# Codebook convolutions on TensorE: softmax numerators in 32-row array tiles, with patches assembled in DRAM

## The chip, the cores and the metric

The kernel runs on one core of a Trainium2 chip, float32 throughout. The metric is the device time of one execution in microseconds (us). Where a kernel ran once, its run's state can't be told; runs of two or more here are in the fast state.

## The reference, cut to what matters

Sixteen images of 256 channels and 28 x 28 pixels go through group norm and two 3 x 3 convolutions in which each channel's patch of nine taps is replaced by a softmax over 16 codes:

```python
p = patches(x)                                  # b, pixel, channel, 9 taps
d = sum(p*p) - 2 * p @ centroids + sum(centroids**2)    # b, pixel, channel, 16 codes
attn = softmax(-d, axis=-1)
lut = einsum('cks,cso->cko', centroids, w_sub)  # channel, code, 256 outputs
out = einsum('bnck,cko->bno', attn, lut)
# conv 1: relu(bn(.)); conv 2: bn, squeeze-excite gate; then relu(out + x); then + x
```

The term |p|^2 is the same for all codes and cancels in the softmax. There are 32 *stages*: 16 images by two convolutions.

## The kernel before

A unit is 8 channels by 448 or 336 pixels. Logits have pixels on the partitions, so the maximum and the sum over the codes are reductions along the free axis. The attention weights must then be transposed before the lookup. Patches go from SBUF to SBUF.

```python
def logits(u):
    for i in range(nt):     # 73 rows: a row of ones, 9 taps x 8 channels
        nc.tensor.matmul(lg[:PP, i * P : (i + 1) * P], lhsT=pt[:, k, c0 : c0 + PP],
                         rhs=wd[l][:, g, :], start=True, stop=True)
    nc.vector.tensor_reduce(mx, lv, axis=AX.X, op=ALU.max)
    nc.vector.tensor_tensor(zv, lv, mx..., ALU.subtract)
    nc.scalar.activation(z, z, AF.Exp, scale=2.0)
def normalise(u):
    nc.vector.tensor_reduce(sm, zv, axis=AX.X, op=ALU.add)
    nc.vector.reciprocal(sm, sm)
    nc.gpsimd.tensor_tensor(zv, zv, sm..., ALU.mult)
def transpose(u):
    for i in range(nt):
        nc.tensor.transpose(tp[:, i * PP : (i + 1) * PP], z[:, i * P : (i + 1) * P], ident[:PP, :PP])
    nc.scalar.copy(at, tp)
def lookup(u):
    for o in range(NB):     # 128 (channel, code) rows against a table made in the setup
        nc.tensor.matmul(acc[o, hi], lhsT=lut[l][:, g, o * P : (o + 1) * P], rhs=u["at"], ...)
# ... cut: setup of the table, norms, gate, the order of the stream
```

## Time and profile before

| | before |
|---|---|
| time | 5238.65 us (two runs, 5236.41 and 5240.88) |
| TensorE busy | 98% |
| DMA engines busy (main queue) | 13.8% |
| DRAM read, written | 17.90 MB, 12.85 MB |

In these lines each digit is a fortieth of the run in tenths, PEclk is the clock granted to TensorE, and the queue's columns are packets, MB and its share of 16 engines' time:

```profile
PEclk9999999999999999999999999999999999999999
DMA  1111111111111111111111111111111111111110
...
q1 hardware_dynamic: 124480, 278.29, 13.8%
...
HBM read 17.90 MB, written 12.85 MB: 6 GB/s over the span
```

The transfers are nearly idle and hardly touch DRAM.

### The profile page before, as it was taken

The numbers are of one execution on the slowest core, as the hardware profiler recorded it, in microseconds if no ns is written. First come the engines' busy times: TensorE is split into PE (matmuls) and PEld (weight loads), VectorE is DVE, ScalarE is ACT, GpSimd is POOL, SyncE is SP. The second block draws the span as 40 slices with busy tenths as digits, with TensorE's granted clock in tenths as the row PEclk, the third lists the DMA queues.
The fourth block names the chain that finished last, engine by engine and source line by source line (L and its number), as shares of the span: only waits on it lengthen the run. The fifth ranks groups of instructions, "written<-read, shape, count | busy, mean of one in ns | idle before, by whom it ended". The sixth has DMA issues, their size and how long they took to land.

```text
span 5236.6 us, 94950 instructions
## 1 busy us (share of the span) xinstructions
PE 5144.1 (98%) x30112; PEld 3875.6 (74%) x30112; DVE 4102.7 (78%) x8497; ACT 2106.5 (40%) x4417; POOL 1944.8 (37%) x2105
## 2 busy tenths in 40 slices
PE   6899999999999999999999999999999999999999
PEld 2677777777777777777777777777777777777776
DVE  1778787878878788787888878788787887878787
ACT  2344434444434444434444444444344444344443
POOL 1333333333333333333333333333333333333333
PEclk9999999999999999999999999999999999999999
DMA  1111111111111111111111111111111111111110
GB/s 40 72 51 49 51 62 51 62 50 62 51 50 62 51 62 50 50 62 51 62 50 59 53 52 61 50 62 51 51 61 50 62 51 51 62 50 56 52 55 37
DMA packets 132931, 284.70 MB, mean 54 GB/s; under 512 B 45904, under 2 KB 50528, under 8 KB 132448
## 3 DMA queue, kind: packets, MB, share of 16 engines
q1 hardware_dynamic: 124480, 278.29, 13.8%
q8 instruction: 258, 4.23, 0.3%
q14 instruction: 225, 1.84, 0.1%
q10 hardware_dynamic: 7968, 0.34, 0.1%
HBM read 17.90 MB, written 12.85 MB: 6 GB/s over the span
## 4 chain that ended last, share of the span: by engine, by line
PE 91%; DVE 3%; DMA 2%; SPq 1%; ACT 1%; issue 1%; ACTq 1%; POOL 0%; DVEq 0%; POOLq 0%
PE acc L341 48%; PE lg L303 28%; PE tp L328 13%; DMA xt<-in_x_dram 2%; SPq L290 1%; PE ps L157 1%; ACT y L365 1%; ACTq L145 1%; DVE sm L320 1%; PE ps L164 1%; DVE mx L310 1%; DVE gn_st L196 0%; DVE z L313 0%; DVE y L275 0%; DVE sm L321 0%
## 5 line engine op out<-in xcount | busy, mean ns | idle before, releaser
L322 POOL TENSOR_TENSOR z<-z,sm 120x512 f32<-120x512 f32 (+1 forms) x2048 | 1904.9, 949 | 3133.2 <-DVE sm L321 2965.0
L341 PE MATMUL acc<-at,lut 128*128 128x448 f32 (+1 forms) x8192 | 2909.7, 494 | 6.4 <-ACT at L330 5.5
L341 PEld LDWEIGHTS acc<-at,lut 128*128 128x128 f32 x8192 | 1457.1, 190 | 885.9 <-issue 680.8
L314 ACT ACTIVATE z<-z 120x512 f32<-120x512 f32 (+1 forms) x2048 | 1087.9, 570 | 1994.2 <-DVE z L313 1960.3
L303 PE MATMUL lg<-wd,pt 73*120 73x128 f32 x14336 | 1765.5, 273 | 15.4 <-DMA pt<-xn 9.9
L310 DVE TENSOR_REDUCE mx<-lg 120x32 f32<-120x512 f32 (+1 forms) x2048 | 1240.6, 622 | 625.5 <-PE lg L303 624.7
L303 PEld LDWEIGHTS lg<-wd,pt 73*120 73x120 f32 x14336 | 1659.7, 183 | 54.0 <-issue 22.4
L320 DVE TENSOR_REDUCE sm<-z 120x32 f32<-120x512 f32 (+1 forms) x2048 | 1188.2, 614 | 345.7 <-ACT z L314 340.3
L330 ACT COPY at<-tp 128x448 f32<-128x448 f32 (+1 forms) x2048 | 916.9, 487 | 962.4 <-PE tp L328 960.6
L313 DVE TENSOR_TENSOR z<-lg,mx 120x512 f32<-120x512 f32 (+1 forms) x2048 | 1179.0, 612 | 2.7
L328 PEld LDWEIGHTS tp<-ident,z 120*128 120x128 f32 x7168 | 826.8, 141 | 287.3 <-issue 56.0
L328 PE MATMUL tp<-ident,z 120*128 120x120 f32 x7168 | 944.0, 266 | 7.2 <-POOL z L322 7.1
L321 DVE RECIPROCAL sm<-sm 120x32 f32<-120x32 f32 (+1 forms) x2048 | 537.9, 298 | 4.0
L157 PE MATMUL ps<-ws,wd 73*128 73x256 f32 x128 | 59.3, 650 | 42.4 <-DMA wd<-in_L_conv_centroids_dram 38.1
L162 DVE TENSOR_TENSOR sq<-wd 73x512 f32<-73x512 f32 x16 | 10.9, 688 | 98.2 <-PE ps L164 77.7
L157 PEld LDWEIGHTS ps<-ws,wd 73*128 73x128 f32 x128 | 33.9, 313 | 68.0 <-issue 44.3
L365 ACT ACTIVATE y<-acc,bnsh,bnsc 128x448 f32<-128x448 f32 (+1 forms) x64 | 42.7, 672 | 25.6 <-PE acc L341 25.6
L358 ACT ACTIVATE h<-acc,bnsh,bnsc 128x448 f32<-128x448 f32 (+1 forms) x64 | 41.6, 678 | 26.5 <-PE acc L341 26.5
L196 DVE BATCH_NORM_STATS2 gn_st<-xt 128x6 f32<-128x392 f32 x64 | 31.6, 555 | 24.4 <-DMA xt<-in_x_dram 24.4
L151 POOL MEMSET ws<- 1x2048 f32 x8 | 14.3, 1794 | 77.3 <-PE ps L157 70.5
L158 ACT COPY lut<-ps 128x256 f32<-128x256 f32 x64 | 23.7, 372 | 36.9 <-PE ps L157 31.0
L275 DVE SCALAR_TENSOR_TENSOR y<-y,se_gt,xn 128x784 f32<-128x784 f32 x32 | 37.8, 1185 | 0.6
(48 smaller groups left out, 236.7 us busy)
## 6 DMA issues: line engine op xcount, KB each, us to landing
pt<-xn SPq DMA_DIRECT2D x2304, 52.5 KB
pt<-h SPq DMA_DIRECT2D x2304, 52.5 KB
xt<-in_x_dram SPq DMA_DIRECT2D x16, 784.0 KB
out_dram<-y SPq DMA_DIRECT2D x16, 784.0 KB
ws<-in_L_conv_wsub_dram SPq DMA_DIRECT2D x72, 64.0 KB
wd<-in_L_conv_centroids_dram ACTq DMA_DIRECT2D x64, 4.5 KB
vecs<-in_L_conv_bn_gamma_dram ACTq DMA_DIRECT2D x2, 1.0 KB
vecs<-in_L_conv_bn_beta_dram ACTq DMA_DIRECT2D x2, 1.0 KB
```

Of the source, the lines that this page charges most:

```text
L157: nc.tensor.matmul(ps, lhsT=wdl[:, g, :], rhs=ws[:, qi, :], start=True, stop=True)
L303: nc.tensor.matmul(lg[:PP, i * P : (i + 1) * P], lhsT=pt[:, k, c0 : c0 + PP], rhs=wd[l][:, g, :], start=True, stop=True,)
L310: nc.vector.tensor_reduce(mx, lv, axis=AX.X, op=ALU.max)
L313: nc.vector.tensor_tensor(zv, lv, mx.unsqueeze(2).to_broadcast([PP, n, K]), ALU.subtract)
L314: nc.scalar.activation(z[:, : nt * P], z[:, : nt * P], AF.Exp, scale=2.0)
L320: nc.vector.tensor_reduce(sm, zv, axis=AX.X, op=ALU.add)
L321: nc.vector.reciprocal(sm, sm)
L322: nc.gpsimd.tensor_tensor(zv, zv, sm.unsqueeze(2).to_broadcast([PP, n, K]), ALU.mult)
L328: nc.tensor.transpose(tp[:, i * PP : (i + 1) * PP], z[:, i * P : (i + 1) * P], ident[:PP, :PP])
L330: nc.scalar.copy(at[:, : nt * PT].rearrange("p (r w) -> p r w", w=W), tp[:, : nt * PP].rearrange("p (r w) -> p r w", w=WP)[:, :, 0:W],)
L341: nc.tensor.matmul(acc[o, hi][:, : nt * PT], lhsT=lut[l][:, g, o * P : (o + 1) * P], rhs=u["at"][:, : nt * PT], start=u["first"], stop=u[" ...
L365: nc.scalar.activation(y[:, o, t0 * PT : (t0 + nt) * PT], a, AF.Identity, bias=sh[:, o : o + 1], scale=sc[:, o : o + 1], accum_out=ysum[:, ...
```

## The change

Its intent is to take TensorE, the bound, out of the transposes and of a third of the lookup's cost. Codes go on the partitions instead of pixels. Three channels (27 taps and helper rows) share a 32-row tile of the array, and eight tiles run at once. The exponentials are multiplied with the centroids to *softmax numerators* (27 taps and three sums in 32 rows), which sub-weights then turn into outputs, four tiles to a 128-row matmul. A maximum over codes now lies across partitions: a first pass of logits is turned in 32 x 32 blocks and reduced, the maxima go through DRAM into spare patch rows, and a second pass of logits subtracts them. The sums go out to DRAM, in again over 128 partitions, through a logarithm and an exponential for the reciprocal, out and in again. Patches are assembled in DRAM: three copies of the image (left, middle, right shift; `home`) are written, and nine transfers copy them into patch order (`pat`), from which tiles are loaded.

The diff, cut to its core (cuts are marked):

```diff
-            nc.tensor.matmul(lg[:PP, i * P : (i + 1) * P], lhsT=pt[:, k, c0 : c0 + PP], rhs=wd[l][:, g, :], ...)
-    nc.vector.tensor_tensor(zv, lv, mx.unsqueeze(2)..., ALU.subtract)
-    nc.tensor.transpose(...)          # and lookup(), the table's setup, im2col() in SBUF
 ...
+    def to_home(l, b, part):
+        if part == 0:
+            nc.sync.dma_start(view(dst, DX + W, [[NPAD, P], [P * NPAD, NB], [1, HW]]), src)
+            return
+        if dx == 0:
+            nc.sync.dma_start(view(dst, to + 1, [[NPAD, P], [W, H], [1, W - 1]]), img[:, :, 0 : W - 1])
+        else:
+            nc.sync.dma_start(view(dst, to, [[NPAD, P], [W, H], [1, W - 1]]), img[:, :, 1:W])
+    def to_pat(l, b, n):
+        nc.sync.dma_start(view(pat_of(l, b), base * HW, [[32 * HW, NRT], [step * HW, 3], [1, HW]]),
+            view(d_home[l], dx * DX + j * NPAD, [[3 * NPAD, NRT], [W, 3], [1, HW]]))
 ...
+    def logits(u, gi, first, rows, n):
+        for i in range(4):
+            for h in range(2):
+                nc.tensor.matmul(bs[i][64 * h : 64 * h + 64, :n],
+                    lhsT=wd[l][32 * i : 32 * i + rows, 2 * g + h, :],
+                    rhs=u["pt"][32 * i : 32 * i + rows, 2 * gi + h, first : first + n], start=True, stop=True)
+    def a_turn(u, gi):                # first pass
+            nc.vector.transpose(z[:, :n], u["lg", gi][i][:, :n])
+    def a_max(u, gi):
+            nc.vector.tensor_reduce(u["mx"]..., z..., axis=AX.X, op=ALU.max)
+    def m_out(u): ...                 # maxima to DRAM
+    def m_in(u): ...                  # and into rows 7, 15, 23 of each tile of pt
+    def b_exp(u, gi):                 # after the second pass
+            nc.scalar.activation(e[:, :n], bk[:, :n], AF.Exp, scale=2.0)
+    def b_num(u, gi):
+                nc.tensor.matmul(bs[h][32 * i : 32 * i + 32, :n], lhsT=cw[l][64 * h : 64 * h + 64, g, i, :],
+                    rhs=e[64 * h : 64 * h + 64, :n], start=True, stop=True)
+    def b_keep(u, gi): nc.scalar.copy(u["q"]..., bk[:, :n])
+    def s_out(u): nc.sync.dma_start(view(u["ds"], ...), u["q"][7::8, :m])
+    def s_in(u):  nc.sync.dma_start(u["sp"][:, :m], view(u["ds"], ...))
+    def r_make(u):
+        nc.scalar.activation(sp, sp, AF.Ln)
+        nc.scalar.activation(sp, sp, AF.Exp, scale=-1.0)
+    def r_out(u): nc.sync.dma_start(view(u["dr"], ...), u["sp"][:, :m])
+    def r_in(u):  nc.sync.dma_start(u["rt"][7::8, :m], view(u["dr"], ...))
+    def c_scale(u, gi):
+            nc.vector.stream_shuffle(rb[:, :n], u["rt"][:, a : a + n], MASK)
+            nc.gpsimd.tensor_tensor(u["q"][:, a : a + n], u["q"][:, a : a + n], rb[:, :n], ALU.mult)
+    def c_look(u, gi, o):
+            nc.tensor.matmul(accs[key][:, :n], lhsT=ws[l][:, 2 * g + h, o * P : (o + 1) * P], rhs=u["q"]..., ...)
 ... cut: the order of the slots, borders, norms, gate, constants
```

A *slot* is 24 channels by 384 or 400 pixels; there are 704. A *unit* of one or two slots is what the round trips work on; there are 384.

## The prediction

> **What bounds the kernel now.** I read the page's busy shares first, then the chain that ended last, then a stretch of that chain in order of time, then the groups.
>
> ```profile
> PE 5144.1 (98%) x30112; PEld 3875.6 (74%) x30112; DVE 4102.7 (78%) x8497; ACT 2106.5 (40%) x4417; POOL 1944.8 (37%) x2105
> PE acc L341 48%; PE lg L303 28%; PE tp L328 13%; DMA xt<-in_x_dram 2%; SPq L290 1%; PE ps L157 1%; ACT y L365 1%; ACTq L145 1%; DVE sm L320 1%; PE ps L164 1%; DVE mx L310 1%; DVE gn_st L196 0%; DVE z L313 0%; DVE y L275 0%; DVE sm L321 0%
> ```
>
> TensorE is both the busiest engine and 91% of the chain. A busy TensorE alone would prove little, but the chain in order of time closes without a gap:
>
> ```profile
> 2501.27 2.63 PE acc L341 x8
> 2503.90 0.72 PE tp L328 x7
> 2504.62 1.53 PE lg L303 x14
> 2506.15 2.64 PE acc L341 x8
> ```
>
> A period (two units: 8 channels, 784 pixels) is 2.63 + 0.72 + 1.53 = 4.88 us, all TensorE; 1,024 periods make 5.00 of the 5.24 ms. The rest is the setup (first logits start at 152 us) and the tail. From these lines come my TensorE rates. A float32 matmul is two instructions (8,192 for 4,096 lookups in the code), and the eight lookup instructions average 392 columns and 329 ns: 0.84 ns a column and instruction. The logits' 14 weight loads and matmuls of 120 to 128 columns go at 109 ns each.
>
> ```profile
> L310 DVE TENSOR_REDUCE mx<-lg 120x32 f32<-120x512 f32 x1024 | 704.5, 688 | 621.8 <-PE lg L303 621.0
> L310 DVE TENSOR_REDUCE mx<-lg 120x24 f32<-120x384 f32 x1024 | 569.3, 556 | 3.7 <-PE lg L303 3.7
> L320 DVE TENSOR_REDUCE sm<-z 120x32 f32<-120x512 f32 x1024 | 700.5, 684 | 330.6 <-ACT z L314 330.0 <-issue 0.2
> L322 POOL TENSOR_TENSOR z<-z,sm 120x384 f32<-120x384 f32 x1024 | 857.8, 838 | 100.3 <-DVE sm L321 41.2 <-PE lg L303 33.0 <-ACT z L314 24.5
> L314 ACT ACTIVATE z<-z 120x384 f32<-120x384 f32 x1024 | 522.0, 510 | 60.9 <-DVE z L313 58.0
> L330 ACT COPY at<-tp 128x336 f32<-128x336 f32 x1024 | 454.3, 444 | 199.1 <-PE tp L328 197.6 <-ACT at L330 0.2
> ```
>
> These give the other engines' costs at about 400 columns (the second number after the bar, in ns). VectorE costs 1.03 ns a column plus about 160 ns. It is second, at 78%: a change that only relieves TensorE can win at most to there.
>
> **What the Trainium skill says.** (1) "TensorE: Matmul & The Clock Gate", Part 3 on row and column tiling: matmuls in distinct tiles of the array run at once; sixteen 32x32 tiles measured 10.6 times. The same part says matmuls are strictly first in, first out in start and end. The trace of before can't confirm either: its large matmuls use 73 rows or more, hence no tiles. (2) "TensorEngine Tiling (Array Packing)", Key Properties: changing the tiling mode drains the engine. No trace here yet. (3) "VectorE: DVE Perf Modes", the perf-mode tier table: tensor_reduce and STREAM_SHUFFLE exist only at one element a cycle. The trace agrees for the reduce (688 ns for 512 columns). (4) "DMA: Bandwidth & Descriptors", anatomy of one DMA: about 2 us are fixed, mostly the write's receipt. The trace's issue and landing records of the patch transfers (52.5 KB) give a median of 2.8 us, so it agrees roughly.
>
> **The change part by part.** The unit of work becomes a slot: 24 channels (eight 32-row tiles of three) by 384 or 400 pixels. 32 stages x 2 pixel tiles x 11 slots = 704 slots. A slot is 1.5 old periods of work (7.33 us of old time). Padding to 264 channels makes the total 1,056 old periods' worth in place of 1,024.
>
> *TensorE, a slot.* Removed: the transposes (0.72 us a period) and the 73-row logits. The table lookup becomes four full 128x128 matmuls (8 instructions of 392 columns): 2.63 us, as eight do now. A table group held 8 channels in 128 rows; numerator rows hold 12 (nine taps each), so this costs 2.63 instead of 3.95 us. Added: logits twice (eight 31x64 tiles each, 400 and 392 columns) and numerators (eight 64x32 tiles): 24 matmuls, 48 instructions of about 0.33 us. One after the other they would be 15.8 us; the change lives on their running at once. If eight tiles run at once, each group takes two passes (0.66 us) or its weight loads, whichever is longer: 16 loads of 64 columns at 0.9 ns (109 ns for 120) are 0.9 us, of 32 columns 0.46 us. I take 1.0, 1.0 and 0.7 us. Four changes of tiling a slot at about 0.16 us (a matmul's 266 ns record less its 103 ns spacing in the transposes: the pipeline's length, an estimate) are 0.65 us. Sum: 2.63 + 2.7 + 0.65 = 6.0 us.
>
> *VectorE, a slot.* Removed: subtraction, sum, reciprocal. Kept: the maxima. Added: a 32x32 block transposition of every logit and the shuffles. Four transpositions of 400 columns from PSUM and four reductions, each 573 ns by the maxima's row, about 555 with the overlap of successors seen in the timeline (a pair takes 1.21 us for 1.24 of records): 4.4 us. Two shuffles at 0.53 us: 1.06. The transposition of the maxima (256 columns, 0.38 us a unit of 1.83 slots): 0.21. Sum 5.7 us; 704 slots make 4.0 ms, and 0.13 ms of norms and residuals stay.
>
> *ScalarE, a slot.* Four exponentials (517 ns at 392 columns), two copies (488 ns), logarithm and exponential for the reciprocal (about 0.4 us): 3.4 us. *GpSimd:* two products at 852 ns: 1.7 us. Neither bounds.
>
> *DMA.* The patch reads stay near 290 MB against 278 now. Assembling the patches in DRAM adds 238 MB (nine transfers of 828 KB a stage). Now 278 MB are 13.8% of the engines; after it perhaps 30%. Small pieces are cheap: 64-byte packets take 10 ns in the setup. What counts is latency: maxima go out and back (two landings), sums out and back, reciprocals out and back (four). At 2.8 us each these need 5.6 us in a window of about 1.6 slots (9.8 us), and 11 us in over four. Both fit, and the ends of the chains stand half a slot apart, which fits landings of 2.8 us and slots near 6 us.
>
> *Sum.* The slot is set by TensorE (6.0) and VectorE (5.7) side by side, with little left for the handover: VectorE must empty four of six banks before the second logits, and ScalarE those before the next first logits. I put 6.1 us on a slot: 704 x 6.1 = 4,294 us. The start (x in, norm, borders, nine assemblies, first patches; no table to make): about 80 us for 152 now. The tail (nine slots of lag with little in them, gate, store): 45 us. **4,420 us.**
>
> **The rivals.**
> *Tiles don't overlap enough.* The two instructions of one float32 matmul use the same tile, so the second must wait for the first. If starts are strictly in order, only the second of one tile overlaps the first of the next: 9 steps in place of 2 for a group, 3 us, and a slot is 3 x 3.0 + 2.63 = 11.6 us: 8.2 to 8.4 ms. For it: the skill's sentence on order. Against: the design itself, which would be pointless (it computes all logits twice), and its lags, which are cut for slots near 6 us. Issue itself is no obstacle:
>
> ```profile
> L243 PE MATMUL ps<-ysum,w_sb x8: 163/163/177, 2543.7 to 2543.9; 128*16 128x1 f32 x8
> ```
>
> Eight one-column matmuls with their loads start within 0.2 us: about 25 ns a pair.
> *VectorE is the bound.* With TensorE at 4.6 us (no load limit, cheap mode changes) the slot is 5.7 us: 4.0 + 0.13 + 0.12 = 4.15 to 4.25 ms. For it: its count is the surest part of the sum.
> *The round trips through DRAM are the bound.* All of them go through one queue that waits in order. The sums' part (out 2.8, in 2.8, reciprocal 1 to 2, out 2.8, in) is about 10 us for each unit of two slots, and an assembly transfer ahead delays it by some 3 us. A slot would then be 7 us and the time 5.0 ms. Against: the queue's parts interleave, and most slots have no assembly.
> *Logarithm and exponential need different tables.* Two loads of 1.28 us (the one in the trace of before) for 384 units are 0.98 ms on ScalarE: 3.4 ms busy. It would lengthen the slot only by its place in the chain, some 0.2 us.
>
> **Range and chances.** Most of the weight lies between the VectorE floor (4.15 ms) and round trips that bite (5.0 ms), so 4,050 to 5,300 us. About one in seven goes to tiles that hardly overlap, which is far outside. Hence faster 0.81, within 2% 0.03, slower 0.16.
>
> **What would show it.** Right: matmul groups of 16 records starting within about 1 us, a VectorE busy above 90%, TensorE's span per slot near 6 us, few waits on DMA. The spacing of successive tiled matmuls decides the first rival: near 60 ns it falls, near 330 ns every second one it holds. A block transposition above 0.6 us would put VectorE above TensorE; idle time of TensorE ended by a DMA before the second logits, or of VectorE before the shuffles, would show the round trips. More than one ACT_TABLE_LOAD shows the tables. The prediction is wrong at its root if the groups take 3 us.

## The result, and the profile after

The kernel after takes 6626.53 us (two runs, 6622.87 and 6630.20), with results that agree with the reference. The ratio to before is 1.265, 95% interval 1.2614 to 1.2687. Ratios are the mean time of one kernel's fast runs over that of the other's of the same rounds, so not quite the ratio of the medians. It is 26% slower, outside the range and in the other direction than predicted.

The page after, answering to the lines shown of before (busy shares, fortieths, queue, DRAM):

```profile
PE 4794.6 (72%) x39692; PEld 1742.8 (26%) x39692; DVE 3781.4 (57%) x9141; ACT 3072.5 (46%) x6034; POOL 1525.5 (23%) x1490
...
PE   0009777778687777977777787877779777777978
...
PEclk5558887889888888988888897887889788788989
DMA  1174777675767767586776758577675867767573
...
q1 hardware_dynamic: 1292484, 872.37, 64.4%
...
HBM read 672.02 MB, written 448.08 MB: 169 GB/s over the span
```

TensorE is now busy 72%, and the clock granted to it is 0.85 in the mean from 600 us on (0.99 in e5_none_one below, where it hardly pauses). No engine is near its limit. The first three digits of TensorE are 0: some 500 us pass before any logits. The main queue moves 3.1 times the bytes and holds the DMA engines 64% of the time. With no engine full, the time must lie in waits, so I looked first at a stretch in order of time, then at the waits in sum. First, one group of first-pass logits by itself (duration in ns as least, median, most; first and last start in us):

```profile
L353 PE MATMUL lg<-pt,wd x16: 481/506/532, 3001.3 to 3001.7; 31*64 31x384 f32 x16
```

Sixteen instructions of half a microsecond start within 0.4 us. The records behind it show eight starts 7 ns apart, then, 327 ns after the last of these, eight more: all first passes of the float32 matmuls, then all second ones. So the tiles do overlap, and the rival that held 14% falls. The stretch around it (start, duration, and in brackets the idle time before with what ended it):

```profile
2996.62 3.01 SPq L445 DMA_DIRECT2D ds<-q  x1
...
3001.28 0.90 PE L353 MATMUL lg<-pt,wd 31*64 31x384 f32 x16
3002.11 1.61 PE L489 MATMUL acc<-q,ws 128*128 128x400 f32 x4
3003.65 0.88 PE L427 MATMUL nm<-e,cw 64*32 64x384 f32 x16
3004.46 0.90 PE L353 MATMUL lg<-pt,wd 31*64 31x384 f32 x16
3005.29 1.61 PE L489 MATMUL acc<-q,ws 128*128 128x400 f32 x4
3008.90 0.34 SPq L450 DMA_DIRECT2D sp<-ds  x1
...
3011.95 0.37 ACT L455 ACTIVATE sp<-sp 128x200 f32<-128x200 f32 x1 [9.96 <-DMA sp<-ds]
...
3014.42 2.70 PE L353 MATMUL lg<-pt,wd 31*64 31x384 f32 x16 [7.52 <-ACT q L440]
```

From start to start, a slot is 0.83 (logits) + 1.54 (half the products with sub-weights) + 0.81 (numerators) + 0.83 + 1.54 = 5.55 us. That is the kernel as designed, better than the 6.1 I gave it. Then it stops. The sums sent out at 2996.62, right behind the last copy of an image, are in DRAM only at 3008.90, twelve microseconds later, where 2.4 us is the median. The packet records show what lay in front of them: the 108-byte packets of that image copy run from 2997.1 to 3005.6 us, and the first packet of the sums starts only at 3002.6. ScalarE has come to the logarithm in its program and waits 9.96 us for them. Behind the logarithm stand the copies and exponentials that empty PSUM banks, so TensorE has nowhere to write and idles 7.52 us; its next group then takes 2.70 us in place of 0.90.

How often that happens shows in the distances between the 704 numerator groups, worked out from the trace: the least 5% are at 5.50 us, the median 6.33, the highest quarter above 10.8, the highest 5% above 19.1, the mean 8.6. So nearly the whole loss is stalls on top of a good slot.

Not all of a stall is idle time. The trace grants TensorE either the full clock or half of it: half for 2,333 us of this run, for 603 us of e5_none_one, the start of some 500 us included in both. Two successive products that start at half clock are 666 ns apart at the median, at full clock 336. TensorE's busy time for the same 39,692 instructions is 4,795 us here and 4,091 there. So up to some 700 us of the loss (an estimate, the difference of these two) is TensorE working slowly, or waiting inside its groups, around stalls. The prediction, whose rates come from a run at a granted clock of 0.999, has no term for this.

The waits (in all, times, longest, in us):

```profile
ACT sp L455 <- DMA sp<-ds: 987.4, 218, 27.3
...
PE lg L353 <- DMA pt<-dm: 651.8, 146, 17.6
...
DVE rb L479 <- DMA rt<-dr: 640.1, 227, 16.4
...
PE lg L353 <- ACT q L440: 407.7, 117, 11.9
```

All three round trips (sums, maxima, reciprocals) are there, each with waits several times a landing. The groups of instructions tell that the engines' own costs are not to blame (the second number after the bar is the mean in ns):

```profile
L480 POOL TENSOR_TENSOR q<-q,rb 128x384 f32<-128x384 f32 (+1 forms) x1408 | 1404.4, 1019 | 4673.6 <-DVE rb L479 2482.8
L369 DVE STREAM_TRANSPOSE z<-lg 128x416 f32<-128x416 f32 (+1 forms) x2816 | 1437.5, 567 | 1552.6 <-PE lg L353 1549.4
...
L377 DVE TENSOR_REDUCE mx<-z 128x26 f32<-128x416 f32 (+1 forms) x2816 | 1394.5, 558 | 0.0
...
L455 ACT ACT_TABLE_LOAD x384 | 492.7, 1283 | 602.5 <-DMA sp<-ds 597.5
L479 DVE STREAM_SHUFFLE rb<-rt 128x384 f32<-128x384 f32 (+1 forms) x1408 | 768.7, 594 | 3.2 <-issue 1.1
```

I had taken 573, 573 and 530 ns for the three VectorE forms and 852 for GpSimd's. The table loads are the rival that I gave 0.2 us a slot: 384 before the logarithm and as many before its exponential, 985 us of ScalarE in all.

Which transfers hold the DMA engines follows from the trace's packet records. The left and right copies of the image write rows of 27 pixels, 108 bytes: 458,752 packets. Half of them take 13 ns or less, but 5% take over 184 and the mean is 46. These 49.5 MB, under 6% of the queue's bytes, are 19.9% of the span of the 16 engines, close to a third of all DMA work. One such copy of 378 KB is in place some 13 us after its issue. The first 500 us have the same look:

```profile
47.07 62.48 ACTq L127 DMA_DIRECT2D home<-zero  x2
126.17 5.58 SPq L263 DMA_DIRECT2D home<-xn  x1
211.05 69.05 ACTq L127 DMA_DIRECT2D home<-zero  x2
402.90 2.80 SPq L112 DMA_DIRECT2D xt<-in_x  x1
```

Border columns are cleared in single elements of 4 bytes, 7,392 to a transfer, and issuing two such transfers takes 62 and 69 us. Their packets go on longer: those of the first two run from about 49 to 192 us, 106 a microsecond over all engines, although the record of one packet is 7 ns long. So the duration of a packet alone doesn't price such a transfer. The image copies wait for the borders, and the load of the second image, which stands behind them in the same queue, is issued at 403 us.

### The profile page after: what moved, and what is told of

Its sections match the earlier page's. It is cut to its first block, busy times and chain, and to the rows that moved or that the text cites. A ratio compares the mean times of both kernels' runs of the same rounds, so it can differ in the third digit from the quotient of the medians.

```text
span 6628.5 us, 106293 instructions
## 1 busy us (share of the span) xinstructions
PE 4794.6 (72%) x39692; PEld 1742.8 (26%) x39692; DVE 3781.4 (57%) x9141; ACT 3072.5 (46%) x6034; POOL 1525.5 (23%) x1490
## 3 DMA queue, kind: packets, MB, share of 16 engines
q1 hardware_dynamic: 1292484, 872.37, 64.4%
## 5 line engine op out<-in xcount | busy, mean ns | idle before, releaser
L489 PE MATMUL acc<-q,ws 128*128 128x384 f32 (+1 forms) x5632 | 2534.8, 577 | 182.6 <-POOL q L480 181.7
L353 PE MATMUL lg<-pt,wd 31*64 31x384 f32 (+2 forms) x22528 | 1769.6, 573 | 1224.9 <-DMA pt<-dm 651.8
L480 POOL TENSOR_TENSOR q<-q,rb 128x384 f32<-128x384 f32 (+1 forms) x1408 | 1404.4, 1019 | 4673.6 <-DVE rb L479 2482.8
L369 DVE STREAM_TRANSPOSE z<-lg 128x416 f32<-128x416 f32 (+1 forms) x2816 | 1437.5, 567 | 1552.6 <-PE lg L353 1549.4
L418 ACT ACTIVATE e<-lg 128x400 f32<-128x400 f32 (+1 forms) x2816 | 1183.8, 517 | 779.0 <-PE lg L353 778.0
L489 PEld LDWEIGHTS acc<-q,ws 128*128 128x128 f32 x5632 | 1063.5, 210 | 1662.7 <-issue 1003.6
L377 DVE TENSOR_REDUCE mx<-z 128x26 f32<-128x416 f32 (+1 forms) x2816 | 1394.5, 558 | 0.0
L440 ACT COPY q<-nm 128x384 f32<-128x384 f32 (+1 forms) x1408 | 608.1, 483 | 934.1 <-issue 647.0
L455 ACT ACT_TABLE_LOAD x384 | 492.7, 1283 | 602.5 <-DMA sp<-ds 597.5
L479 DVE STREAM_SHUFFLE rb<-rt 128x384 f32<-128x384 f32 (+1 forms) x1408 | 768.7, 594 | 3.2 <-issue 1.1
L427 PE MATMUL nm<-e,cw 64*32 64x384 f32 (+1 forms) x11264 | 676.6, 539 | 1.9 <-ACT se_hid L297 1.9
L456 ACT ACT_TABLE_LOAD x384 | 492.7, 1283 | 6.8
```

The lines of the kernel that those rows point to most:

```text
L353: nc.tensor.matmul(bs[i][64 * h : 64 * h + 64, :n], lhsT=wd[l][32 * i : 32 * i + rows, 2 * g + h, :], rhs=u["pt"][32 * i : 32 * i + rows, ...
L369: nc.vector.transpose(z[:, :n], u["lg", gi][i][:, :n])
L377: nc.vector.tensor_reduce(u["mx"][:, 4 * gi + i].rearrange("p (c b) -> p b c", c=2)[:, : n // 32], z[:, :n].rearrange("p (b c k) -> p b c ...
L418: nc.scalar.activation(e[:, :n], bk[:, :n], AF.Exp, scale=2.0)
L427: nc.tensor.matmul(bs[h][32 * i : 32 * i + 32, :n], lhsT=cw[l][64 * h : 64 * h + 64, g, i, :], rhs=e[64 * h : 64 * h + 64, :n], start=True ...
L440: nc.scalar.copy(u["q"][:, (2 * gi + h) * n : (2 * gi + h + 1) * n], bk[:, :n])
```

## The experiments

Theory: the mean slot grew because assembling the patches in DRAM, through its small pieces, delays the landings of the round trips, and an in-order ScalarE passes each delay on to TensorE. Rivals: the table loads lengthen the chain of the sums; the single in-order queue, not the DMA engines, delays the landings; the order of the transfers does; the round trips are too long by themselves. The start is a separate term. Slots below are mean distances of the 704 numerator groups. Letters stand for chips; which chip the first measurement used is not on record. Runs without n are single executions, whose state is unknown: a difference between them and runs on another chip can come from the chip or from that one execution.

| run | chip | edit | time, us | slot, us |
|---|---|---|---|---|
| after | first | none | 6626.53 (n=2) | 8.64 |
| e1_no_assembly | A | no assembly | 5146.39 | 6.51 |
| e2_whole_rows | A | shifted copies as whole rows | 5786.84 | 7.42 |
| e3_one_table | A | no table loads | 6544.48 | 8.51 |
| e4_act_queue | A | assembly on another queue | 6755.84 | 8.81 |
| e5_none_one | B | no assembly, one table | 4671.68 | 5.86 |
| e6_retimed | B | assembly spread out | 6443.27 | 8.37 |
| e8_local | C | sums stay on the chip, one table | 6014.13 | 7.77 |
| e9_start | D | borders by whole rows | 6588.70 | 8.95 |
| f1_after | E | none | 6621.77 (n=2) | 8.62 |
| f2_start | E | as e9_start | 6348.35 (n=2) | 8.64 |
| f3_one_table | E | as e3_one_table | 6313.47 (n=2) | 8.19 |
| f4_retimed | E | as e6_retimed | 6441.28 (n=2) | 8.38 |
| g1_after | F | none | 6622.45 (n=2) | 8.63 |
| g2_whole_rows | F | as e2_whole_rows | 5698.16 (n=2) | 7.33 |
| v1 | B | a version, below | 5194.14 | 7.19 |
| v2 | C | a version, below | 4910.77 | 6.78 |
| v3 | C | a version, below | 4810.01 | 6.65 |
| v3_timed | D | v3 again | 4816.59 (n=4) | 6.66 |

The kernel before took 5235.8 to 5243.5 us beside all of these.

### e1_no_assembly

The transfers are left out; all stages read old patches, so the numbers are wrong on purpose.

```diff
     def pat_of(l, b):
-        if l == 0: return d_pat[2 if b == 1 else 0]
-        return d_pat[0 if b == B - 1 else 1]
+        return d_pat[2 if (l, b) == (0, 1) else 0]
     def prep(l, b, t, near):
+        return
```

> Edit: after the first two images nothing is assembled in DRAM any more, later stages read the first image's patches again (wrong numbers on purpose). Theory A (the round trips of maxima and sums wait behind the assembly's transfers, in the same queue): nearly all slots take the 5.6 us that undisturbed slots of the changed kernel take, so 500 us of start + 704 x 5.6 + 40 = about 4,500 us. Theory B (the two table loads of each unit stall ScalarE, the assembly is incidental): the time falls by less than 400 us, to above 6,200 us. Theory C (the round trips are too long for their lags even alone): slots stay uneven, 5,200 us or more.

Measured: 5146.39 us, some 1,480 us less (across chips), between the marks of theories A and C, with TensorE's busy time above 90% in nearly every slice after the start. Busy shares, fortieths and the queue, then two of the waits:

```profile
PE 4359.4 (85%) x39692; PEld 1603.5 (31%) x39692; DVE 3785.6 (74%) x9141; ACT 3072.3 (60%) x6034; POOL 1527.3 (30%) x1490
...
PE   0000999999999999999999999999999999999998
...
q1 hardware_dynamic: 778074, 578.28, 41.4%
...
ACT sp L453 <- DMA sp<-ds: 364.6, 244, 4.3
...
PE lg L351 <- DMA pt<-dm: 72.9, 97, 3.1
```

ScalarE's wait for the sums falls from 987 to 365 us and TensorE's for the maxima from 652 to 73, although both round trips are untouched. So it is the assembly that delays the round trips. They don't quite fit by themselves: the slot is 6.51 us in the mean, with 5% above 10.2. e5_none_one looks at that rest.

### e2_whole_rows

The shifted copies are written as unshifted whole rows of 3,136 bytes: the same bytes within 4%, no 108-byte pieces after the first two images (28,672 of 458,752 stay), wrong numbers on purpose.

```diff
-            nc.sync.dma_start(view(dst, to + 1, [[NPAD, P], [W, H], [1, W - 1]]), img[:, :, 0 : W - 1])
+        nc.sync.dma_start(view(dst, to, [[NPAD, P], [1, HW]]), src[:, k])
```

> Edit: the four column-shifted copies of each image into DRAM are written as whole unshifted rows (3,136-byte pieces in place of 108-byte pieces, 4 percent more bytes, wrong numbers on purpose). If the small pieces are what holds the queue (these copies land after 13 us now): they land after about 4 us and the time falls by half or more of the assembly's cost, to 5,000 to 5,700 us. If it is the number of bytes or the place in the queue of any assembly transfer: above 6,200 us.

Measured: 5786.84 us, just above the theory's bracket. The copies land in 3.8 us instead of 13. So the pieces, not the bytes, are the larger part of the assembly's cost: 840 of the 1,480 us, both across chips. How large is settled by g2_whole_rows.

### e3_one_table

The logarithm becomes a scaled copy, so that no table changes (wrong numbers).

```diff
-        nc.scalar.activation(sp, sp, AF.Ln)
+        nc.scalar.activation(sp, sp, AF.Copy, scale=0.1)
```

> Edit: the logarithm of the sums becomes a scaled copy, which needs no other table (wrong numbers on purpose). Theory A: ScalarE loses 985 us of table loads, but the waits behind the assembly stay; the time falls by 100 to 400 us, to 6,200 to 6,500 us. Theory B: the time falls by about 1,000 us or more, to 5,700 us or less.

Measured: 6544.48 us, 82 us below the first measurement of after. I read that as tables being worth next to nothing while the assembly is there. That reading was wrong by a factor of nearly four, because it set one execution on chip A against runs on another chip; see f3_one_table.

### e4_act_queue

The assembly is issued by ScalarE instead of SyncE, so that it has a queue of its own. The results are correct.

```diff
-            nc.sync.dma_start(view(dst, ...), ...)
+            eng.dma_start(view(dst, ...), ...)        # eng = nc.scalar within the stages
```

> Edit: in the steady state the assembly's transfers are issued by ScalarE on its own DMA queue, same transfers, same result. Theory A with the order in the queue as the cause: the round trips no longer stand behind them, landings of the sums' transfers come down from up to 19 us to 2 to 5 us, time 5,000 to 5,700 us. If the shared DMA engines or memory are the limit rather than the order: above 6,200 us.

Measured: 6755.84 us. The landings on the round trips' own queue, with no image copy in front of them, still reach 17 to 19 us (the sums out 17.4, the reciprocals out 19.1 at most). So the delay arises in the shared DMA engines; the queue's order isn't needed for it. Whether the own queue gains or loses a little here is open: no unedited run was made on chip A.

### e5_none_one

Both suspects out: e1_no_assembly, and one table set named at the start (wrong numbers because of the former).

```diff
+    nc.scalar.preload_act_table_set("natural_log_exp_and_others")
```

> Edit: as the run without assembly, and in addition the table set that holds both logarithm and exponential is loaded once at the start (wrong numbers on purpose, from the missing assembly only). The run without assembly left slots of 6.4 us on average against 5.55 undisturbed, and the queue waiting 1,535 us for the reciprocals on ScalarE. If the tables cause that rest: slots of 5.6 us, about 530 + 704 x 5.6 + 40 = 4,510 us. If it is the length of the round trips themselves: 4,900 us or more.

Measured: 4671.68 us, between the two marks and nearer to that of the tables: a slot of 5.86 with a median of 5.58, and one table load in place of 769.

```profile
PE 4090.9 (88%) x39692; PEld 1492.8 (32%) x39692; DVE 3769.1 (81%) x9141; ACT 2115.0 (45%) x5265; POOL 1527.1 (33%) x1491
```

The design, without the start, the assembly and the table loads, keeps the slot that was predicted for it (6.1 us). Against e1_no_assembly the tables are worth 475 us; as the chips differ and both ran once, a difference like the 89 us between g2_whole_rows and e2_whole_rows may be in it.

### e6_retimed

The assembly's transfers are spread over the stage and set right after the maxima's; the results are correct.

```diff
-            at(t + 3 + (i // 2 if near else i), 8, to_pat, l, b, i)
+            at(t + SPOT[near][i], 5, to_pat, l, b, n)     # SPOT: slots 4 to 15
```

> Edit: the same assembly, spread over the stage: each transfer is issued right behind the maxima's return instead of right ahead of their way out, copies earlier in the stage (right numbers). If what hurts is only that the maxima's way out stands behind an assembly transfer: a gain of 500 us or more, to 6,100 us or less. If the copies of 108-byte pieces hold the DMA engines for 13 us and more wherever they stand: 6,300 to 6,600 us.

Measured: 6443.27 us, 183 us less. Repeated as f4_retimed.

### e8_local

The sums no longer go through DRAM: the shuffle takes them from the numerators themselves, and ScalarE does logarithm and exponential of all 400 columns, with one table set. The assembly and the start are untouched; the results are correct.

```diff
-            nc.vector.stream_shuffle(rb[:, :n], u["rt"][:, a : a + n], MASK)
+            nc.vector.stream_shuffle(rb[:, :n], u["q"][:, a : a + n], MASK)
+            nc.scalar.activation(rb[:, :n], rb[:, :n], AF.Ln)
+            nc.scalar.activation(rb[:, :n], rb[:, :n], AF.Exp, scale=-1.0)
 ... s_out, s_in, r_make, r_out and r_in are removed
```

> Edit to the changed kernel: the sums make no round trip; VectorE's shuffle takes them straight from the numerator rows, ScalarE inverts the shared-out sums (logarithm and exponential of 400 columns, four a slot in place of two of 200 a unit), one table set; assembly and start as they were (right numbers). ScalarE then has about 5.1 us a slot. If the sums' chain is what stands behind the assembly most: 5,300 to 5,800 us. If the maxima's chain alone is held up as much: 6,200 us or more.

Measured: 6014.13 us, 612 us less than after (across chips), between the two brackets, so a miss for both. One table is worth 308 us by itself (f3_one_table), so taking four landings out of the chain is worth about 300 with the assembly in place: an estimate, as the edit also adds activations and the two gains need not add up. TensorE's wait for the maxima stays (658.3 us for 651.8): that round trip goes on being delayed.

### e9_start

One edit in the start: each image copy in DRAM is cleared by one transfer of whole rows.

```diff
-            nc.scalar.dma_start(view(t, 0, [[NPAD, 3 * CPAD], [29 * W, 2], [1, W]]), zeros(...))
-            nc.scalar.dma_start(view(t, C * NPAD, ...), zeros(...))
-            for dx, col in ((0, 0), (2, W - 1)):
-                nc.scalar.dma_start(view(t, dx * DX + W + col, [[NPAD, CPAD], [W, H], [1, 1]]), zeros(...))
+            nc.scalar.dma_start(view(t, 0, [[NPAD, 3 * CPAD], [1, NPAD]]), zeros([[0, 3 * CPAD], [1, NPAD]]))
```

> The kernel after with one edit at the start: the image copies in DRAM are cleared by one transfer of whole 3,360-byte rows each, in place of four kinds of border transfers of which two move single 4-byte elements. Slots are untouched. Theory (the start is long because the first copies of the image wait for the 4-byte border transfers): the first logits move from about 501 us to 150 to 230 us, and the whole time falls by as much, to 6,260 to 6,370 us, with the mean slot still 8.6 us. Rival (the start is bound by the loads and the first nine patch transfers, which share the engines): first logits no earlier than 400 us and the time above 6,500 us.

Measured: 6588.70 us, a miss for the theory. The numerators start 263 us earlier, but the time falls by 38 us only: the mean slot is 8.95 for 8.64 us. A tempting story is that the gain was given back. The packets speak against it. The 108-byte ones took 53.1 ns in the mean, for 45.9 in after, 52.0 in e3_one_table and 40.3 in e6_retimed; so part of every comparison across chips may be the chip, or the one execution on it. The next four runs put the unedited kernel and three edits on one chip.

### f1_after, f2_start, f3_one_table, f4_retimed

> The kernel after, unedited, as a baseline on the chip that the next three runs share. If chips differ in how fast they write small pieces, its time differs from the 6,627 us of the first measurement by up to 4% and follows its own mean time of a 108-byte packet: above 6,700 us if that mean is near 53 ns, near 6,627 if near 46, near 6,450 if near 40. If chips don't differ, 6,627 within 0.5% whatever the packets do.

Measured: 6621.77 us, 46.1 ns a packet: the same as the first measurement.

> The same edit as in e9_start (image copies cleared by whole rows). Theory (the chip made e9_start's slots longer, not the edit): 230 to 290 us less than f1_after on this chip, with the same mean slot within 0.05 us. Rival (the edit itself makes the slots longer, or a shorter start is given back later): less than 100 us of gain, with a mean slot 0.2 to 0.35 us above that of f1_after.

Measured: 6348.35 us, 273 us less at an unchanged slot (8.64 for 8.62 us), as the theory said. The start in order of time:

```profile
5.04 2.05 ACTq L124 DMA_DIRECT2D home<-zero  x2
72.20 0.39 SPq L258 DMA_DIRECT2D home<-xn  x1
...
226.76 5.17 PE L348 MATMUL lg<-pt,wd 31*64 31x384 f32 x40 [77.34 <-DMA pt<-pat]
```

The first image copy goes out at 72 instead of 126 us, the first logits start at 227 instead of 502. So nothing is given back: e9_start's longer slots came from its chip or from its one execution, which the record can't tell apart. The edit also took away border rows of 112 bytes; by the packets above, the 4-byte ones took most of the time.

> The logarithm replaced by a scaled copy (wrong numbers on purpose), so that no table is loaded in the slots, as in e3_one_table. Against f1_after on the same chip: 80 to 250 us less if the loads sit mostly in ScalarE's waiting time while the assembly is there; 400 to 500 us less if they cost as much as they did with the assembly gone (475 us between e1_no_assembly and e5_none_one).

Measured: 6313.47 us, 308 us less, between the two brackets, so a miss for both. It is 231 us less than the identical kernel took on chip A.

```profile
PE 4619.2 (73%) x39692; PEld 1668.2 (26%) x39692; DVE 3770.5 (60%) x9141; ACT 2106.8 (33%) x5266; POOL 1525.9 (24%) x1490
```

ScalarE loses 965 us of busy time, and the run gains a third of that: about two thirds of the loads lay in time in which ScalarE waited anyway. With the assembly gone, and that waiting with it, the same loads cost 385 to 475 us (e5_none_one).

> Assembly transfers spread over the stage, as in e6_retimed. Against f1_after on the same chip: 0 to 100 us less if most of e6_retimed's 183 us came from its chip; 150 to 250 us less if the order of the transfers itself is worth that.

Measured: 6441.28 us, 180 us less, as in e6_retimed. The mean 108-byte packet is 40.2 ns here too, so that figure came from the edit and not from a chip. The order of the transfers is a real but small part.

### g1_after, g2_whole_rows

> The kernel after, unedited, as the baseline of this chip: 6,600 to 6,640 us if its mean 108-byte packet is near 46 ns as on two chips so far, some 6,850 if it is near 52 to 53 as on two others.

Measured: 6622.45 us, 46.0 ns a packet.

> The shifted image copies written as unshifted whole rows of 3,136 bytes (wrong numbers on purpose), as in e2_whole_rows: no 108-byte pieces, the same bytes within 4%. If the slowness of a chip lies in those small pieces alone, this kernel takes 5,790 us within 1% on any chip, and what it is worth against g1_after is 810 to 850 us on a chip with 46 ns or some 1,060 on one with 53 ns. If the chips differ in all transfers alike, its time differs by 2% or more from 5,787 in the direction of g1_after's.

Measured: 5698.16 us, 924 us less on the same chip. It is 1.5% less than e2_whole_rows took on chip A, between the brackets: small pieces are not all in which that execution on chip A was slower. The page of this run, busy shares and queue:

```profile
PE 4629.5 (81%) x39692; PEld 1691.3 (30%) x39692; DVE 3783.5 (66%) x9141; ACT 3070.2 (54%) x6034; POOL 1525.8 (27%) x1490
...
q1 hardware_dynamic: 877764, 874.09, 50.3%
```

The queue moves as many bytes as in after (874.09 for 872.37 MB). The landing of the sums that only 5% exceed falls from 13.3 us (g1_after) to 5.2, and that of the reciprocals from 11.6 to 4.9. The largest single part of the stalls, 924 of 2,161 us (summed up below), is thus shown by taking away the pieces alone.

### v1, v2, v3: the versions they point to

v1 keeps the results right and takes the pieces away: GpSimd shifts the image in SBUF, and whole rows are written. It has one table set, the retimed assembly, and a start with zero sources in SBUF and later loads of what the first stage doesn't need. It also has four patch buffers for five, and loads patches somewhat later.

```diff
+        if dx == 0:
+            nc.gpsimd.tensor_copy(tgt[:, :, 1:W], img[:, :, 0 : W - 1])
+        else:
+            nc.gpsimd.tensor_copy(tgt[:, :, 0 : W - 1], img[:, :, 1:W])
+        nc.sync.dma_start(view(dst, dx * DX + k * P * NPAD + W, [[NPAD, P], [1, HW]]), sh)
 ... and the edits of e5_none_one (table), e6_retimed, and of the start
```

> Edit: all remedies at once, right numbers: GpSimd makes the column-shifted images in SBUF, so that whole rows go to DRAM; one table set; assembly spread as in the retimed run; the start without border elements of 4 bytes, second image and second layer's weights later. Theory A: start about 110 us, slots 5.7 to 6.3 us, so 4,150 to 4,600 us. If whole rows still cost what the run with whole rows left over the run without assembly (640 us): 4,900 to 5,100 us.

Measured: 5194.14 us, the first numerators at 111 us, a slot of 7.19. The time is above both brackets: the start is as expected, the slot is not. ScalarE still waits 1,204 us for the sums.

v2 is v1 with the assembly issued by ScalarE as in e4_act_queue:

> Edit to the version with all remedies: its assembly is issued on ScalarE's queue (right numbers). That version spent 1,411 us of the in-order queue waiting for the reciprocals to land, behind 830 KB transfers. If with large pieces the order in the queue is what is left: 4,600 to 4,900 us. If the engines serve both queues alike and the landings stay: 5,100 us or more.

Measured: 4910.77 us, just above the first bracket. With the slow pieces gone, the order in the one queue does matter: 283 us on another chip (v1 has no 108-byte pieces, and this comparison wasn't repeated on one chip).

v3 is v1 with the sums kept on the chip as in e8_local, and lags of 4, 5 and 8 slots for 3, 4 and 9:

> Edit to the version with all remedies: the sums are inverted on the chip as in the local run, and the second logits come one slot later (right numbers). Only the maxima go through DRAM, with two and a half slots for it. Slots of 5.7 to 6.2 us as ScalarE (5.2), VectorE (5.4) and TensorE (5.3) are all nearly full: 4,150 to 4,500 us. If assembly still holds up the maxima: above 4,700 us.

Measured: 4810.01 us, in the bracket of "assembly still holds up the maxima". That isn't the reason, though: in v3_timed TensorE waits 2 us in all for the maxima, for 652 in after.

> The version that the experiments led to (whole-row copies from images shifted on GpSimd, one activation table, sums shared out on the chip, assembly spread out, start mended), now timed in rounds against the kernel before. A single run gave 4,810 us. If that holds: 4,790 to 4,830 us in fast runs, 8 to 8.5% faster than before, with results that agree with the reference.

Measured: 4816.59 us, median of four runs (4808.46 to 4823.46). The ratio to before is 0.9192, interval 0.9177 to 0.9208: 8% faster, with correct results, the fastest correct version.

```profile
PE 4634.6 (96%) x39696; PEld 1774.8 (37%) x39696; DVE 3769.0 (78%) x9143; ACT 3169.1 (66%) x7313; POOL 1625.0 (34%) x1620
```

TensorE is busy 96% of the span again, but not full: nearly the same instructions took 4,091 us in e5_none_one, at the same granted clock of 0.99 in the slots, so some 540 us of this busy time (an estimate, the difference) are waits inside its groups. Its slot is still 6.66 and not 5.55 us; four more activations a slot are among what it now has to wait for. How much could be had there is open.

## Why the prediction was wrong

By its own steps:

- *TensorE, a slot: 6.0 us.* Right in kind and somewhat too long: 5.55 us, with changes of tiling in it. Each tiled group takes 0.81 to 0.83 us from its start to the next group's, where I had 0.7 to 1.0 plus 0.16 for the change. That the sum came so close is partly luck: the products with sub-weights take 2 x 1.54 = 3.08 us for my 2.63, and the three tiled groups 2.47 for 3.35.
- *VectorE 5.7 us, ScalarE 3.4, GpSimd 1.7.* VectorE's busy time is 3,781 us over 704 slots, 5.4 with the norms in it. ScalarE's is 3,073, 4.4 with the 1.4 us of table loads; GpSimd's 1,526, 2.2. Right as costs to within about half a microsecond a slot (ScalarE without the table loads); none sets the slot. VectorE is not "busy above 90%", which I named as a sign, but 57%: the sign fails for the same reason as the sum.
- *Tiles don't overlap enough.* This rival fell by the mark I had set for it. The 0.16 that I gave to "slower" stood mostly for it, so that "slower" came true is no merit of the prediction.
- ***"At 2.8 us each these need 5.6 us ... and 11 us in over four. Both fit."* This is the step that failed.** At their medians the landings do take 1.7 to 4.3 us and would fit. But the term had no place for what else is in the DMA engines. I put the assembly down as bytes ("238 MB", "perhaps 30%"), and not even all of them: by the sizes on the page the round trips move 222 MB and the image copies 75, so the queue moves 872 MB where my terms make 528. And I said "small pieces are cheap: 64-byte packets take 10 ns in the setup". That was the wrong sample: the setup of before wrote its 64-byte pieces into SBUF, the assembly writes 108-byte pieces into DRAM. They take 46 ns, the engines are busy 64%, and landings of sums, reciprocals and maxima reach 19.4, 17.9 and 9.4 us. My rival "the round trips through DRAM are the bound" had the mechanism (an assembly transfer delays the chain) with a delay of "some 3 us" for one of 10 or more, and so a slot of 7 for one of 8.6.
- *Log and exp need different tables, "some 0.2 us".* Happened, and was mis-sized: 308 us over 704 slots are 0.44 us a slot with the assembly there, up to 0.67 without.
- *The start: about 80 us.* Mis-sized: first logits at 502 us. I listed borders and priced them at nothing; clearing them in whole rows gives 273 us back, and v1 shows first logits at 88. That is a mis-sizing by the same blind spot, for most of the time went to pieces of 4 bytes.

The sum closes. From 4,420 us: the undisturbed slot is 0.55 us shorter than assumed (-387 us over 704), the start is some 420 us longer, and stalls of 8.62 - 5.55 = 3.07 us a slot add 2,161. That makes 6,614, for 6,622 measured in f1_after. Of the stalls, whole rows take away 924 us, one table 308 and the order 180, each alone. These need not add up, as a stall can have two causes. Without assembly and tables 0.3 us a slot are left (e5_none_one). What the assembly costs without the 108-byte pieces, some 640 us between e2_whole_rows and e1_no_assembly on chip A, was not taken apart.

On small pieces, the Trainium skill, "DMA: Bandwidth & Descriptors", Specifications, gives at least 512 bytes as the transfer for line rate and says that below this the engine reads, modifies and writes. I had the page open for its fixed cost and didn't carry this row into the sum. It gives the direction, no time. The trace agrees as far as the 108-byte packets go; whether reading and writing back is what makes them slow, no run shows. It also shows 128-byte packets, the maxima on their way out to DRAM, at 14.7 ns in the mean; so size alone doesn't decide, and whether the alignment of the 108-byte pieces does was not tried. The fixed 2 us that the prediction took from the same page are told there of transfers that GpSimd issues; here SyncE issues them, and the shortest landings of the round trips are 1.5 to 2.1 us. Naming a joint set follows the same skill's "ScalarE: Activation LUTs", Table sets: the hidden batching unit, by which exponential and logarithm are both in one set and need one load. The trace agrees once the set is named (one load in e5_none_one).

## What to carry to other kernels

When a change moves work from a full engine to transfers, count the pieces and where they are written, not the bytes, and price them by a sample of the same direction and size, by landings and not by packets alone; if the profile before holds none, the range has to be wide on that side. Here a chain of short transfers was as long as its slowest landing beside everything else in the DMA engines, and ScalarE, working in order, handed each late landing to all that stood behind it. Repeat the unedited kernel on the same chip before believing a difference of a few per cent: here one and the same program took 231 us more in one execution on one chip than in two on another, while the kernel before differed by 0.15%.

## What the Trainium skill lacked or had wrong

- "DMA: Bandwidth & Descriptors", Specifications: no time is given for writing pieces below 512 bytes to DRAM. Here 108-byte writes to DRAM took 13 ns at the median and 46 in the mean, with 5% above 184, and raised the landings of other transfers from about 2 us to as much as 19. Clearing columns in 4-byte elements went at 106 pieces a microsecond, about 140 us per two transfers of 7,392, with 7 ns on the record of each packet.
- "TensorE: Matmul & The Clock Gate", Part 3: its sentence on strict first-in, first-out order made me fear that the two instructions of a float32 matmul would serialise the tiles. Here eight tiles of float32 start 7 ns apart and their second instructions 327 ns later, 16 in 0.90 us. The page doesn't say how the two instructions of a float32 matmul go with tiles.
- "ScalarE: Activation LUTs", What ACT_TABLE_LOAD costs: it gives about 1,283 ns for the load, as all 769 here took, and about 1,380 ns more for a drain, 2.66 us in all. The drain isn't seen here: at the median an activation starts 11 ns after a load, and a load 18 ns after an activation.
- The same page, Table sets: it has logarithm and then exponential needing one load; without naming the set this kernel got two a unit.
- No page says how far runs of a kernel that hangs on transfers can differ: with the copies' order untouched, the mean 108-byte packet took 46 to 48 ns in runs on chips C, E and F and 50 to 53 in single executions on A and D, and the same program took 6313.47 us on E and 6544.48 on A. Whether chip or execution differs is not shown.
